# A pair-product batch norm on one core: joining two neighbouring short rows in one tile, beside two long rows in one space of 152 pairs

## The chip, the cores and the metric

The kernel runs on one core of one Trainium2 chip. The time is the device time of that core in microseconds, the median of several runs. The kernel before takes 1864.45 us (three runs, 1864.28 to 1864.72); its profiled run has a span of 1862.7 us. A core has five engines that the profile names: PE (TensorE, matrix products), DVE (VectorE), ACT (ScalarE), POOL (GpSimd) and SP (SyncE, which here only issues transfers), and 16 DMA engines that move data between HBM and the on-chip memory.

## The reference

There are two inputs, xi and xj, each of 1024 samples, 39 fields and 16 numbers. A *pair* (r, c) has a row r from 1 to 38 and a column c from 0 to r - 1, 741 in all; row r has r pairs. For each pair and sample the outer product of xj[r] and xi[c] is formed, 16 x 16 numbers. It is normalised with the mean and variance of that pair over all samples, scaled by gamma and beta, and multiplied by a 16 x 16 weight W:

```python
_ROWS, _COLS = np.tril_indices(39, k=-1)
cross = xj[:, rows, :, None] * xi[:, cols, None, :]
mean = jnp.mean(cross, axis=(0, 2, 3), keepdims=True)
var = jnp.mean(jnp.square(cross - mean), axis=(0, 2, 3), keepdims=True)
normed = (cross - mean) * jax.lax.rsqrt(var + BN_EPS)
normed = normed * gamma[None, :, None, None] + beta[None, :, None, None]
out = normed[:, :, None, :, :] * W[None, None, :, :, :]
return jnp.transpose(out, (0, 2, 1, 3, 4))
```

The output has 1024 x 741 x 256 float32 numbers, 777 MB. In it the pairs of a row follow each other, and row r + 1 follows row r, so for one sample a row is one run of r KB, and two neighbouring rows are one run too.

## The kernel before, in words

**Layout.** A partition of the 128 holds 8 samples (NT = 8). A tile is one row r for T = 2 of them: 2r pairs of 256 numbers, so 2r KB in each partition. All output passes through one buffer, y_sb, of 152 pairs (152 KB in each partition), cut in two halves of 76 (`half`). A tile is laid out sample by sample: the r pairs of sample 0, then the r pairs of sample 1.

**Order of the tiles** (the list `tiles`, lines 68 to 77; an entry is row, first sample, place in y_sb). First row 19, four tiles of 38 pairs. Then row 20, then rows 38 down to 21. A long row r and its partner, the short row 38 - r, have 38 pairs together and fill one half: the long tile at the start of the half, the short one behind it. The halves take turns. So the order is long, short, long, short, and a place is used again after one further half.

**Statistics.** Sums and products of sums over all samples give mean and variance of all pairs without forming the outer products; this takes the first 25 us or so and is not touched. It leaves for each pair a factor s and an offset t, in groups of rows (`ROW_GROUPS`; `apply` prepares a group when a given tile is reached).

**One tile.** `scale_xi` (line 164, POOL) multiplies the r columns of xi by s. `products` (line 178) forms the outer products: for a long enough row one instruction for each sample and each of the 16 values i of xj, most of them on ACT (12 of 16, or 13, or 11 for rows over 33) and the others on POOL, all at line 148 or 150. Rows 5 to 7 are done by POOL in one instruction for each sample (line 203), rows 1 to 4 by DVE (lines 183 and 193). `finish` (line 271) adds t and multiplies by W, one DVE instruction for each pair and both samples (line 308); POOL does a share of the pairs (lines 294 and 297, for rows over 33 with ACT's help at line 292). `store` (line 220) issues the transfers, line 231, all from SP. Rows of up to 19 pairs leave as one transfer for both samples. Longer ones leave as one transfer for each sample; rows over 30 send the first sample in two pieces, the first when its pairs are done (`bounds`, line 262); rows 37 and 38 send the first piece for both samples at once.

**What sets the order.** The program's own order on each engine, written out by the loop at line 521: for tile n it emits `scale_xi` of n + 2, `finish` of n and `products` of n + 1. An instruction that writes pairs of y_sb waits until the earlier transfers that read those same pairs have landed. That is how a new tile waits for the old contents of its place, sample by sample: the places, not the order alone, decide which transfers it waits for.

Of the kernel before, what the change touches and what calls it, by code (L numbers as in the profile page):

```python
# [7 lines left out]
F32 = mybir.dt.float32  # L8
# [6 lines left out]
T = 2  # L15
# [16 lines left out]


ROW_GROUPS = (
    (19, 20, 0, None), (20, 21, 1, None), (18, 19, 1, 2), (38, 39, 1, 8), (34, 38, 1, 9), (1, 5, 1, 10), (29, 34, 2, 36),
    (5, 10, 2, 37), (25, 29, 3, 76), (10, 14, 3, 77), (21, 25, 4, 108), (14, 18, 4, 109),
)
SHORT_GROUP = 5

# [2 lines left out]
def tile_pair_outer_batchnorm(  # L42
# [24 lines left out]

    half = T * (F - 1)
    mid = (F - 1) // 2
    tiles = [(mid, t0, t0 // T * half // 2) for t0 in range(0, NT, T)]  # L70
    slot = 0
    for r in (mid + 1, *range(F - 1, mid + 1, -1)):
        for t0 in range(0, NT, T):
            tiles.append((r, t0, slot * half))
            if r < F - 1:
                tiles.append((F - 1 - r, t0, slot * half + T * r))
            slot ^= 1

    RAW = 1

# [55 lines left out]
    stt = nc.vector.scalar_tensor_tensor  # L136

    def view(n):
        r, _, u = tiles[n]
        return y_sb[:, u : u + T * r, :].rearrange("p (t n) e -> p t n e", t=T)  # L140

    def product(n, engine, t, i, src):

        r, t0, _ = tiles[n]
        y = view(n).rearrange("p t n (i j) -> p t n i j", j=E)[:, t, :, i, :]
        scale = xj_sb[:, t0 + t, r, i : i + 1]
        if engine is nc.scalar:
            nc.scalar.activation(y, src, AF.Copy, scale=scale)  # L148
        else:
            engine.tensor_scalar(y, src, scale, 1.0, ALU.mult, ALU.mult)  # L150

    def raw_products(n, engine, steps):
        r, t0, _ = tiles[n]
        for step in steps:
            t, i = divmod(step, E)
            yield lambda t=t, i=i: product(n, engine, t, i, xi_sb[:, t0 + t, 0:r, :])

    def emit(work, count):
        for _, step in zip(range(count), work):
# [2 lines left out]
    xs_of = {}  # L162

    def scale_xi(n):
        r, t0, _ = tiles[n]
        if r <= SHORT:
            return
        n0 = first[r]
        xs = scaled.tile([P, T, r, E], F32, tag="xs", name=f"xs_{r}_{t0}")
        nc.gpsimd.tensor_tensor(  # L170
            xs,
            xi_sb[:, t0 : t0 + T, 0:r, :],
            s_sb[:, :, n0 : n0 + r, :].to_broadcast([P, T, r, E]),
            ALU.mult,
        )
        xs_of[n] = xs

    def products(n):

        r, t0, _ = tiles[n]  # L180
        if r <= SHORT:
            xs = scaled_short.tile([P, T, r, E], F32, tag="xs_short", name=f"xs_{r}_{t0}")
            nc.vector.tensor_tensor(  # L183
                xs,
                xi_sb[:, t0 : t0 + T, 0:r, :],
                s_short[:, first[r] : first[r] + r]
                .unsqueeze(1)
                .unsqueeze(3)
                .to_broadcast([P, T, r, E]),
                ALU.mult,  # L190
            )
            for t in range(T):
                nc.vector.tensor_tensor(  # L193
                    view(n)[:, t].rearrange("p n (i j) -> p n i j", j=E),
                    xs[:, t].unsqueeze(2).to_broadcast([P, r, E, E]),
                    xj_short[:, t0 + t, r - 1 : r, :].unsqueeze(3).to_broadcast([P, r, E, E]),
                    ALU.mult,
                )
            return
        xs = xs_of.pop(n)  # L200
        if r <= OUTER:
            for t in range(T):
                nc.gpsimd.tensor_tensor(  # L203
                    view(n)[:, t].rearrange("p n (i j) -> p n i j", j=E),
                    xs[:, t].unsqueeze(2).to_broadcast([P, r, E, E]),
                    xj_sb[:, t0 + t, r : r + 1, :].unsqueeze(3).to_broadcast([P, r, E, E]),
                    ALU.mult,
                )
            return
        if n < 3:  # L210
            split = E - POOL_I_FIRST[n]
        elif r > LONG:
            split = E - POOL_I_LONG
        else:
            split = E - (POOL_I_BESIDE if SHORT < F - 1 - r <= OUTER else POOL_I)
        for t in range(T):
            for i in range(E):
                product(n, nc.scalar if i < split else nc.gpsimd, t, i, xs[:, t])

    def store(n, c0, c1, t_from=0, t_to=T):  # L220
        r, t0, _ = tiles[n]
        n0 = first[r]

        whole = n >= len(FIRST_PIECES) and r <= WHOLE
        step = 1 if r > mid and (whole or c1 == r) else t_to - t_from
        for t in range(t_from, t_to, step):
            if whole and step == 1 and t == t_to - 1:
                if c1 < r:
                    continue
                c0 = 0  # L230
            nc.sync.dma_start(  # L231
                out_v[:, t0 + t : t0 + t + step, (n0 + c0) * EE : (n0 + c1) * EE],
                view(n)[:, t : t + step, c0:c1, :].rearrange("p t n e -> p t (n e)"),
            )

    def affine(n, pairs, engines=(nc.scalar, nc.gpsimd)):

        r = tiles[n][0]
        y = view(n)
        for c in pairs:  # L240
            s_c = st_sb[:, 0, first[r] + c : first[r] + c + 1]
            t_c = t_sb[:, first[r] + c : first[r] + c + 1]
            engine = engines[c % len(engines)]
            if engine is nc.scalar:
                nc.scalar.activation(y[:, :, c, :], y[:, :, c, :], AF.Identity, bias=t_c, scale=s_c)  # L245
            else:
                engine.tensor_scalar(y[:, :, c, :], y[:, :, c, :], s_c, t_c, ALU.mult, ALU.add)  # L247
# [14 lines left out]
    def bounds(n):  # L262
        if n < len(FIRST_PIECES):
            return FIRST_PIECES[n]
        r = tiles[n][0]
        if r <= ONE:
            return 0, r

        return 0, r // 2 + max(0, (WHOLE + 1 - r) * 3 // 2), r

    def finish(n):


        r = tiles[n][0]
        n0 = first[r]
        y = view(n)
        long = r > LONG
        p1 = r // 2 if long else r
        if long:
            share = POOL_PAIRS_LONG  # L280
        elif RAW < n < 10:
            share = POOL_PAIRS_FIRST
        else:
            share = int(r * POOL_SHARE + 0.5) if r > SHORT else 0
        p0 = p1 - share
        step = POOL_PAIRS_LONG // 2 if long else r
        for c0 in range(p0, p1, step):
            c1 = min(c0 + step, p1)
            for c in range(c0, c1):
                t_c = t_sb[:, n0 + c : n0 + c + 1]  # L290
                if long:
                    nc.scalar.activation(y[:, :, c, :], y[:, :, c, :], AF.Identity, bias=t_c)  # L292
                else:
                    nc.gpsimd.tensor_scalar(  # L294
                        y[:, :, c, :], y[:, :, c, :], t_c, 1.0, ALU.add, ALU.mult
                    )
            nc.gpsimd.tensor_tensor(  # L297
                y[:, :, c0:c1, :],
                y[:, :, c0:c1, :],
                w_sb.unsqueeze(1).to_broadcast([P, T, c1 - c0, EE]),  # L300
                ALU.mult,
            )

        size = 1 if n == RAW else T
        for t in range(0, T, size):
            for c0, c1 in zip(bounds(n), bounds(n)[1:]):
                for c in [*range(c0, min(c1, p0)), *range(max(c0, p1), c1)]:
                    stt(  # L308
                        y[:, t : t + size, c, :],
                        y[:, t : t + size, c, :],  # L310
                        t_sb[:, n0 + c : n0 + c + 1],
                        w_dve.to_broadcast([P, size, EE]),
                        ALU.add,
                        ALU.mult,
                    )
                store(n, c0, c1, t, t + size)

    with tc.manual_schedule():
# [159 lines left out]
        used = [0] * len(ps_st)  # L478

        def spread(group):  # L480
            r0, r1, bank, _ = ROW_GROUPS[group]
            n0, n1 = first[r0], first[r1 - 1] + r1 - 1
            at = used[bank]
            used[bank] = at + 2 * (n1 - n0)
# [33 lines left out]
        products(1)  # L518
        scale_xi(2)

        for n in range(1, len(tiles)):
            if n + 2 < len(tiles):
                scale_xi(n + 2)
            finish(n)
            for group, (_, _, _, tile_of) in enumerate(ROW_GROUPS):
                if n == tile_of:
                    apply(group)
            if n + 1 < len(tiles):
                products(n + 1)
            if n == 12:  # L530
                nc.scalar.copy(xj_short, xj_sb[:, :, 1 : SHORT + 1, :])
# [28 lines left out]
```

## Time and profile before

| | kernel before |
|---|---|
| time, median of 3 | 1864.45 us |
| span of the profiled run | 1862.7 us |
| DVE busy | 1714.3 us, 92% |
| ACT busy | 1576.3 us, 85% |
| POOL busy | 1542.9 us, 83% |
| written to HBM | 776.99 MB |
| DMA packets | 55286, mean 421 GB/s |
| ACT at line 148 waiting for a transfer out | 181.6 us, 82 times |

The page cuts the span in 40 slices of 46.6 us. A digit is the busy share of an engine, or of the 16 DMA engines, in tenths; the row GB/s is what the DMA moved. In the waits, a line says who waited for whom, the sum in us, how often, and the longest. In the timeline a line has the start, the length, the engine, the line, the operation with its shapes and how many instructions are merged; what stands in brackets is the idle time before it and who ended it. A packet is one run of bytes that one DMA engine moves, here nearly always one run of one sample.

### The profile page before, as it was taken

The numbers are of one execution on the slowest core, as the hardware profiler recorded it, in microseconds if no ns is written. First come the engines' busy times: TensorE is split into PE (matmuls) and PEld (weight loads), VectorE is DVE, ScalarE is ACT, GpSimd is POOL, SyncE is SP. The second block draws the span as 40 slices with busy tenths as digits, with TensorE's granted clock in tenths as the row PEclk, the third lists the DMA queues.
The fourth block names the chain that finished last, engine by engine and source line by source line (L and its number), as shares of the span: only waits on it lengthen the run. The fifth ranks groups of instructions, "written<-read, shape, count | busy, mean of one in ns | idle before, by whom it ended". The sixth has DMA issues, their size and how long they took to land.

```text
span 1862.7 us, 9385 instructions
## 1 busy us (share of the span) xinstructions
PE 34.3 (2%) x212; PEld 33.7 (2%) x212; DVE 1714.3 (92%) x2638; ACT 1576.3 (85%) x3130; POOL 1542.9 (83%) x1655
## 2 busy tenths in 40 slices
PE   7000000000000000000000000000000000000000
PEld 7000000000000000000000000000000000000000
DVE  8999889899999999999999999999999999999994
ACT  8999888888888776666898989999999998989891
POOL 9999777787777789999988888888888888888882
PEclk7555555555555555555555555555555555555555
DMA  7999999999999999999999999999999999999998
GB/s 289 396 421 421 430 427 427 429 424 427 424 428 423 424 424 426 427 425 425 420 428 429 428 430 427 426 427 427 427 431 427 426 428 431 428 425 428 428 428 359
DMA packets 55286, 783.60 MB, mean 421 GB/s; under 512 B 4784, under 2 KB 6448, under 8 KB 18096
## 3 DMA queue, kind: packets, MB, share of 16 engines
q1 hardware_dynamic: 54928, 782.53, 99.2%
q14 instruction: 69, 0.57, 0.1%
q10 hardware_dynamic: 288, 0.48, 0.1%
q8 instruction: 1, 0.02, 0.0%
HBM read 6.00 MB, written 776.99 MB: 420 GB/s over the span
## 4 chain that ended last, share of the span: by engine, by line
DMA 53%; ACT 22%; DVE 18%; issue 3%; POOL 1%; PE 0%; SPq 0%; ACTq 0%; DVEq 0%; POOLq 0%
DMA out_dram<-y_sb 53%; ACT y_sb L148 22%; DVE y_sb L308 17%; POOL y_sb L150 1%; DVE y_sb L364 0%; POOL xs L170 0%; POOL y_sb L247 0%; PE ps L401 0%; SPq L231 0%; DVE y_sb L254 0%; ACTq L148 0%; PE ps L379 0%; DVE y_sb L385 0%; DVE y_sb L371 0%; DVE xs L183 0%
## 5 line engine op out<-in xcount | busy, mean ns | idle before, releaser
L308 DVE SCALAR_TENSOR_TENSOR y_sb<-y_sb,st_sb,w_dve 128x512 f32<-128x512 f32 (+1 forms) x2511 | 1653.1, 740 | 113.3 <-issue 95.9
L148 ACT ACTIVATE y_sb<-xs,xj_sb 128x144 f32<-128x144 f32 (+23 forms) x2930 | 1453.0, 586 | 238.2 <-DMA out_dram<-y_sb 181.6
L297 POOL TENSOR_TENSOR y_sb<-y_sb,w_sb 128x2048 f32<-128x2048 f32 (+3 forms) x155 | 517.4, 3343 | 89.1 <-ACT y_sb L292 79.5
L150 POOL TENSOR_SCALAR y_sb<-xs,xj_sb 128x320 f32<-128x320 f32 (+19 forms) x1006 | 557.4, 577 | 9.8 <-DMA out_dram<-y_sb 9.7
L170 POOL TENSOR_TENSOR xs<-xi_sb,st_sb 128x640 f32<-128x640 f32 (+33 forms) x135 | 183.9, 1362 | 178.8 <-ACT y_sb L148 174.5
L294 POOL TENSOR_SCALAR y_sb<-y_sb,st_sb 128x512 f32<-128x512 f32 x291 | 196.8, 692 | 5.1 <-ACT y_sb L148 5.1
L292 ACT ACTIVATE y_sb<-y_sb,st_sb 128x512 f32<-128x512 f32 x160 | 100.2, 708 | 3.8 <-POOL y_sb L150 2.1
L203 POOL TENSOR_TENSOR y_sb<-xs,xj_sb 128x1280 f32<-128x1280 f32 (+2 forms) x24 | 66.7, 2802 | 0.0
L193 DVE TENSOR_TENSOR y_sb<-xs,ps 128x256 f32<-128x256 f32 (+3 forms) x32 | 24.8, 818 | 0.5
L487 PE MATMUL ps<-y_sb 38*128 38x38 f32 (+37 forms) x76 | 16.4, 397 | 2.4 <-DVE y_sb L473 2.4
L487 PEld LDWEIGHTS ps<-y_sb 38*128 38x128 f32 x76 | 16.3, 329 | 2.5 <-POOL y_sb L150 2.5
L150 POOL TENSOR_SCALAR y_sb<-xi_sb,xj_sb 128x304 f32<-128x304 f32 x24 | 11.9, 514 | 0.0
L254 DVE TENSOR_TENSOR y_sb<-y_sb,w_dve 128x2048 f32<-128x2048 f32 (+4 forms) x6 | 10.8, 1840 | 0.5 <-POOL y_sb L247 0.5
L364 DVE TENSOR_REDUCE y_sb<-y_sb 128x38 f32<-128x608 f32 x14 | 10.4, 781 | 0.0
L247 POOL TENSOR_SCALAR y_sb<-y_sb,st_sb 128x512 f32<-128x512 f32 x9 | 7.0, 786 | 2.2 <-ACT y_sb L148 2.2
L245 ACT ACTIVATE y_sb<-y_sb,st_sb 128x512 f32<-128x512 f32 x9 | 6.5, 803 | 0.3 <-ACT y_sb L148 0.3
L361 ACT ACTIVATE y_sb<-xi_sb 128x608 f32<-128x608 f32 x8 | 5.7, 707 | 1.1 <-DMA xi_sb<-in_r_xi_dram 0.7
L361 ACT ACTIVATE y_sb<-xj_sb 128x608 f32<-128x608 f32 x8 | 5.7, 708 | 1.1 <-DMA xj_sb<-in_r_xj_dram 0.6
L379 PE MATMUL ps<-xi_sb,y_sb 128*128 128x152 f32 x40 | 6.1, 302 | 0.0
L379 PEld LDWEIGHTS ps<-xi_sb,y_sb 128*128 128x128 f32 x40 | 5.8, 202 | 0.0
L401 PE MATMUL ps<-y_sb 128*128 128x128 f32 x24 | 5.5, 428 | 1.0 <-POOL y_sb L319 1.0
L401 PEld LDWEIGHTS ps<-y_sb 128*128 128x128 f32 x24 | 5.2, 331 | 1.0 <-POOL y_sb L319 1.0
(43 smaller groups left out, 50.5 us busy)
## 6 DMA issues: line engine op xcount, KB each, us to landing
out_dram<-y_sb SPq DMA_DIRECT2D x16, 3072.0 KB, 21.9
out_dram<-y_sb SPq DMA_DIRECT2D x20, 2432.0 KB, 12.5
out_dram<-y_sb SPq DMA_DIRECT2D x10, 4608.0 KB, 15.2
out_dram<-y_sb SPq DMA_DIRECT2D x12, 3840.0 KB, 20.8
out_dram<-y_sb SPq DMA_DIRECT2D x16, 2816.0 KB, 22.1
out_dram<-y_sb SPq DMA_DIRECT2D x12, 3584.0 KB, 22.9
out_dram<-y_sb SPq DMA_DIRECT2D x12, 3328.0 KB, 24.3
out_dram<-y_sb SPq DMA_DIRECT2D x15, 2560.0 KB, 12.3
```

The costliest lines, as they stand in the source:

```text
L148: nc.scalar.activation(y, src, AF.Copy, scale=scale)
L150: engine.tensor_scalar(y, src, scale, 1.0, ALU.mult, ALU.mult)
L170: nc.gpsimd.tensor_tensor(xs, xi_sb[:, t0 : t0 + T, 0:r, :], s_sb[:, :, n0 : n0 + r, :].to_broadcast([P, T, r, E]), ALU.mult,)
L193: nc.vector.tensor_tensor(view(n)[:, t].rearrange("p n (i j) -> p n i j", j=E), xs[:, t].unsqueeze(2).to_broadcast([P, r, E, E]), xj_short ...
L203: nc.gpsimd.tensor_tensor(view(n)[:, t].rearrange("p n (i j) -> p n i j", j=E), xs[:, t].unsqueeze(2).to_broadcast([P, r, E, E]), xj_sb[:, ...
L292: nc.scalar.activation(y[:, :, c, :], y[:, :, c, :], AF.Identity, bias=t_c)
L294: nc.gpsimd.tensor_scalar(y[:, :, c, :], y[:, :, c, :], t_c, 1.0, ALU.add, ALU.mult)
L297: nc.gpsimd.tensor_tensor(y[:, :, c0:c1, :], y[:, :, c0:c1, :], w_sb.unsqueeze(1).to_broadcast([P, T, c1 - c0, EE]), ALU.mult,)
L308: stt(y[:, t : t + size, c, :], y[:, t : t + size, c, :], t_sb[:, n0 + c : n0 + c + 1], w_dve.to_broadcast([P, size, EE]), ALU.add, ALU.mult,)
L361: nc.scalar.activation(squares[x][:, t], sources[x][:, t], AF.Square, scale=scales[x])
L379: nc.tensor.matmul(ps, unit, sources[x][:, t0:t1, :, e : e + q], start=e == 0, stop=e + q == E)
L487: nc.tensor.matmul(ps[:, :, first[r] - n0 : first[r] - n0 + r], pick[:, r - 1, :], stq[:, :, 0:r], start=True, stop=True,)
```

## The change

From row 37 down the tiles go in rounds of three for each two samples: the long row r (r odd), the long row r - 1, and one tile of both their partners, the short rows 38 - r and 39 - r, which are neighbours. A round has 2r + 2(r - 1) + 2(77 - 2r) = 152 pairs, the whole of y_sb: r at the start, r - 1 at the end, the joined tile between them. The joined tile leaves as one run of 77 - 2r pairs for each sample, where two rows left as two runs. Rows 20, 18 and 38 stay as they were. Row 21, which is left over, goes with row 17, two tiles of each at a time. The aim is fewer and longer runs in the stores. In the functions an entry of `tiles` now holds a tuple of rows, `parts` walks through them, `bounds` gives a joined tile one piece, POOL's share of pairs is taken of the joined tile's sum, and the tiles at which `apply` runs are worked out instead of listed.

```diff
-    tiles = [(mid, t0, t0 // T * half // 2) for t0 in range(0, NT, T)]
+    tiles = [((mid,), t0, t0 // T * half // 2) for t0 in range(0, NT, T)]
     slot = 0
-    for r in (mid + 1, *range(F - 1, mid + 1, -1)):
+    for r in (mid + 1, F - 1):
         for t0 in range(0, NT, T):
-            tiles.append((r, t0, slot * half))
+            tiles.append(((r,), t0, slot * half))
             if r < F - 1:
-                tiles.append((F - 1 - r, t0, slot * half + T * r))
+                tiles.append(((F - 1 - r,), t0, slot * half + T * r))
             slot ^= 1
+    for r in range(F - 2, mid + 2, -2):
+        for t0 in range(0, NT, T):
+            tiles.append(((r,), t0, 0))
+            tiles.append(((r - 1,), t0, 2 * half - T * (r - 1)))
+            tiles.append(((F - 1 - r, F - r), t0, T * r))
+    r = mid + 2
+    for t0 in range(0, NT, 2 * T):
+        tiles.append(((r,), t0, 0))
+        tiles.append(((r,), t0 + T, 2 * half - T * r))
+        tiles.append(((F - 1 - r,), t0, T * r))
+        tiles.append(((F - 1 - r,), t0 + T, T * (F - 1)))
...
     def view(n):
-        r, _, u = tiles[n]
-        return y_sb[:, u : u + T * r, :].rearrange("p (t n) e -> p t n e", t=T)
+        rows, _, u = tiles[n]
+        return y_sb[:, u : u + T * sum(rows), :].rearrange("p (t n) e -> p t n e", t=T)
+
+    def parts(n):
+        at = 0
+        for r in tiles[n][0]:
+            yield r, at, at + r
+            at += r
...
+        for r, c0, c1 in parts(n):
...
             for t in range(T):
-            for i in range(E):
-                product(n, nc.scalar if i < split else nc.gpsimd, t, i, xs[:, t])
+                for i in range(E):
+                    engine = nc.scalar if i < split else nc.gpsimd
+                    product(n, r, c0, engine, t, i, xs[:, t, c0:c1])

     def store(n, c0, c1, t_from=0, t_to=T):
-        r, t0, _ = tiles[n]
-        n0 = first[r]
+        rows, t0, _ = tiles[n]
+        n0, r = first[rows[0]], sum(rows)
...
-        r = tiles[n][0]
-        if r <= ONE:
+        rows = tiles[n][0]
+        r = sum(rows)
+        if r <= ONE or len(rows) > 1:
             return 0, r
...
-            share = int(r * POOL_SHARE + 0.5) if r > SHORT else 0
+            share = int(r * POOL_SHARE + 0.5) if rows[-1] > SHORT else 0
...
+        due = {}
+        for group, (r0, r1, _) in enumerate(ROW_GROUPS[2:], 2):
+            use = min(n for n, tile in enumerate(tiles) if any(r0 <= r < r1 for r in tile[0]))
+            due.setdefault(use - 3 if group == 2 else use - 4, []).append(group)
```

## The prediction

> **What bounds the kernel now.** I read the busy times and the slices of the page first, then the waits, then two DMA windows, then the timeline of single tiles.
>
> ```profile
> PE 34.3 (2%) x212; PEld 33.7 (2%) x212; DVE 1714.3 (92%) x2638; ACT 1576.3 (85%) x3130; POOL 1542.9 (83%) x1655
> ...
> DMA  7999999999999999999999999999999999999998
> GB/s 289 396 421 421 430 427 427 429 424 427 424 428 423 424 424 426 427 425 425 420 428 429 428 430 427 426 427 427 427 431 427 426 428 431 428 425 428 428 428 359
> ...
> HBM read 6.00 MB, written 776.99 MB: 420 GB/s over the span
> ```
>
> DVE's 92% is not the limit: from the second slice to the last but one the DMA row is full, at 420 to 431 GB/s. 777 MB must leave, so the stores set the end. The waits agree: the engines wait for landed stores, not the stores for a late engine.
>
> ```profile
> ACT y_sb L148 <- DMA out_dram<-y_sb: 181.6, 82, 6.7
> POOL xs L170 <- ACT y_sb L148: 174.5, 67, 6.3
> DVE y_sb L308 <- issue: 95.9, 66, 5.0
> ```
>
> So the change can act in two ways: cheaper bytes on a full DMA, or a DMA that runs empty. For the first, compare the DMA between 312 and 915 us (rows 37 to 31, whose first sample leaves in two pieces) with that between 930 and 1830 us (rows 30 to 21, whole runs):
>
> ```profile
> DMA packets 18561, 256.80 MB, mean 426 GB/s; under 512 B 1664, under 2 KB 2432, under 8 KB 8832
> ...
> DMA packets 21715, 385.01 MB, mean 428 GB/s; under 512 B 1856, under 2 KB 1856, under 8 KB 1856
> ```
>
> Leaving out the completion packets of 4 B (under 512 B), these are 65.8 packets per MB at 2.348 us per MB against 51.6 at 2.338. The slope is 0.74 ns of the whole DMA per packet (11.9 ns on one of 16 engines), the rest 2.299 us per MB, 435 GB/s.
>
> For the second, the timeline of ACT, with long tiles of rows 31 and then 30:
>
> ```profile
> 841.56 7.90 ACT L148 ACTIVATE y_sb<-xs,xj_sb 128x496 f32<-128x496 f32 x13 [6.74 <-DMA out_dram<-y_sb]
> 850.71 7.89 ACT L148 ACTIVATE y_sb<-xs,xj_sb 128x496 f32<-128x496 f32 x13 [1.24 <-DMA out_dram<-y_sb]
> 864.41 7.90 ACT L148 ACTIVATE y_sb<-xs,xj_sb 128x496 f32<-128x496 f32 x13 [5.82 <-DMA out_dram<-y_sb]
> 873.69 7.90 ACT L148 ACTIVATE y_sb<-xs,xj_sb 128x496 f32<-128x496 f32 x13 [1.37 <-DMA out_dram<-y_sb]
> ```
>
> One tile is two lines, one for each sample. ACT computes sample 0 (7.9 us) as soon as the old sample 0 of that place has landed, and waits only 1.2 to 1.4 us more for the old sample 1. **Half of the products are hidden under the landing of the second sample.** That matters because little else is spare: the trace puts the issues of the first piece of rows 33 to 30 only 2.4 to 4.3 us before the preceding store lands.
>
> **The Trainium skill.** "DMA: Bandwidth & Descriptors", section "Where 436 GB/s comes from", gives 435.2 GB/s as the ceiling of the SBUF ports; my fit gives 435, the run 428. The same page, "Why small descriptors are slow", has a fixed overhead per packet; the fit agrees in kind, 11.9 ns. Its section "Why a DMA increments its semaphore by 16 and not by 1" says that only the full count means that all has landed, so a waiter is released by the slowest of 16 engines; here 12 engines end at 1854.5 us and the last at 1861.1. "Latency and other measured facts" has some 0.6 us to the first byte of a store from these queues; here the first store's data started 0.9 us after its issue, and the last store landed 0.43 us after its last byte.
>
> **Prices from the trace.** ACT L148 start to start: 0.305 us at 9 pairs, 0.319 at 10, 0.532 at 26, 0.559 at 28, 0.572 at 29, 0.586 at 30, 0.613 at 32, 0.639 at 34. A DVE L308 step takes 0.658 us. A store lands 0.3085 us after the one before it for each pair of a sample (24 pairs in 7.41 us).
>
> ```profile
> 1511.33 18.52 DVE L308 SCALAR_TENSOR_TENSOR y_sb<-y_sb,st_sb,w_dve 128x512 f32<-128x512 f32 x28
> 1511.70 19.68 ACT L148 ACTIVATE y_sb<-xs,xj_sb 128x224 f32<-128x224 f32 x44
> ```
>
> **The change part by part.** Call the three tiles of a round A (row r), B (row r-1) and C (the two short rows), and a stage the four rounds of one r.
>
> 1. *Joined runs.* In eight stages each sample has one short packet where it had two: 8 x 1024 = 8192 packets fewer, x 0.74 ns = 6.1 us. 20 stores fewer, each with a 9 ns completion packet per engine: 0.2 us. Upper end 6.3. Lower end 0: the slowest engine's landings take 93.8 us per 304 pairs in both windows. But that engine also carries 8 KB instruction packets of 0.31 us, more of them in the second window, so I take 6 us.
>
> 2. *Same engine work.* Instruction counts hardly move (four DVE steps more, four POOL ones fewer, 24 fewer POOL multiplications in L297). Engines wait for stores; I cost this at nothing.
>
> 3. *C as one tile.* Its products can't start before its store has landed (both samples in one store up to 19 pairs, row after row above). In the stage 29/28 the chain is: C landed, products of rows 9 and 10 (24 x 0.305 + 24 x 0.319 = 15.0), products of A (24 x 0.572 = 13.7), its 25 DVE steps (16.4), 1.7 us of latencies: 46.8 us. Available: one round, 152 pairs, 46.7 to 46.9. So no margin, 0 to 1.4 us lost twice; I take 1. For 23/22 the same sum leaves about 5 us.
>
> 4. *The place of B.* A starts at 0 and shrinks within its old place, but B ends at 152: it starts at 152 - 2(r-1), and from stage to stage its start moves up by 4 pairs. Old row 36: sample 0 in pairs 80 to 116, sample 1 to 152. New row 34: sample 0 in pairs 84 to 118. **The new sample 0 lies 2 pairs deep in the old sample 1.** In the built program the first product of row 34 indeed waits for the stores of pairs 80-99, 99-116 and 116-152, while later rounds wait only for their own sample; the same for rows 32, 30, 28, 26, 24, 22. So in the first round of a stage nothing of B is computed until all of the old B has landed. Behind the waiting ACT instruction stand C and the next A; POOL's share of B waits too, then DVE, then the store queue.
>
> Count from the landing of the old B. The DMA still has the old C and the new A: W. B needs its products P, the DVE (or, for row 34, L292 and POOL) part F of its first store, and 1.67 us of latencies (landing 0.43, starts 0.2, issue 0.14, first byte 0.9).
> - Row 34: W = 76 x 0.3085 = 23.4; P = 22 x 0.639 = 14.1; F = 4 x 0.613 + 2 x 4.48 (L297) = 11.4. Empty 3.7.
> - Row 32: W = 80 pairs, 24.7; P = 26 x 0.613 = 15.9; F = 23 x 0.658 = 15.1. Empty 8.1.
> - Row 30: W = 84 pairs, 25.9; P = 24 x 0.586 = 14.1; F = 26 x 0.658 = 17.1. Empty 6.9.
> - Row 28: W = 88 pairs, 27.1; 13.4 + 15.8. Empty 3.7.
> - Row 26: W = 92 pairs, 28.4; 12.8 + 15.1. Empty 1.2.
> - Rows 24 and 22: 2 and 5 us to spare. Row 36: the old row 38 stores its first 19 pairs for both samples at once and has the overlap anyway; nothing new.
>
> Sum 23.6 us. The same arithmetic on the kernel before (row 23: 12.3 us of slack worked out, 12.1 in the trace) holds, but for rows 30 to 33 it is 0.2 to 1.2 us too kind, so I add 2: 25.6. Bounds 21 to 29.
>
> Sum: -6 + 1 + 25.6 = +20.6: 1864.45 + 20.6 = **1885**.
>
> **The rivals.** (a) *Faster*: the DMA stays full at the turns of stage and only the packets count: 1864.45 - 6 = 1858.5. For it speaks the full DMA row; against it the waits of the built program, and that the stores of the kernel before have little lead. 6%. (b) *Half*: part of the empty time is caught up, 12 us lost and 6 gained: 1870. Against it: nothing but A and C is queued. 9%, of which 4% so close to the time before that it counts as the same. (c) *The joined C becomes the bound*: step 3 fails by 2 us in each round of the last four stages, and the turns come on top: 1885 + 30 = 1915, or with half of it 1900. Against it: 3 us or more of margin outside 29/28. 7%. My forecast has 78%.
>
> The range takes in the bounds of the two unknown costs: gain 6.3 and loss 21 to 22 give 1879, gain 0 and loss 29 give 1893; a bit of (b) moves the lower end to 1875. Faster 0.06, same 0.04, slower 0.90.
>
> **What will show it.** Right: DMA gaps of 4 to 9 us just ahead of the first store of rows 34, 32, 30 and 28, and after ACT has waited for a store at the start of those tiles with no second wait between the samples; DMA full in between, with about a quarter fewer packets per MB and some 1.5 GB/s more. Wrong: a full DMA row with no gaps (a), or gaps in every round of the late stages (c). The prediction falls if stores land earlier than I reckon at the turn, or if packets turn out to cost the slowest engine nothing.

## The result and the profile after

The changed kernel takes **1892.14 us** (median of four runs, 1891.93 to 1892.22) against 1864.37 us for the kernel before on the same chip: a ratio of 1.0149, interval [1.0131, 1.0167]. That is 27.8 us slower; the forecast was 1885, 20.6 us slower.

First the page of the changed kernel, with the same rows as were shown of before.

```profile
PE 33.1 (2%) x212; PEld 32.3 (2%) x212; DVE 1714.0 (91%) x2642; ACT 1572.9 (83%) x3130; POOL 1530.2 (81%) x1627
...
DMA  7999999999899989998999899999999999999999
GB/s 296 396 422 424 425 426 415 428 428 432 363 433 422 427 342 429 425 423 360 433 429 426 383 421 428 419 414 428 430 429 423 431 429 430 408 428 429 428 428 388
DMA packets 46774, 783.60 MB, mean 415 GB/s; under 512 B 4464, under 2 KB 5104, under 8 KB 12656
```

No engine has more to do: DVE has 1714.0 us where it had 1714.3. But the DMA row has four 8s, and the GB/s row falls to 363, 342, 360 and 383 in just these slices, four apart. A slice is 47.3 us and a stage of four rounds of 152 pairs about 190 us, so the holes come once in a stage. Between them the rate is 422 to 433, about what it was.

The next view is a table by stretches: after the start and end come length, busy time of PE, PEld, DVE, ACT and POOL, granted clock, DMA share and GB/s. The stretches are the holes, found in the records of the packets, and one of 100 us well away from them.

```profile
476.00:482.00 6.00, 0.00 (x0) 0.00 (x0) 6.00 (x10) 6.00 (x11) 6.00 (x3) 0.50 0.15 65
668.00:678.00 10.00, 0.00 (x0) 0.00 (x0) 10.00 (x16) 10.00 (x17) 10.00 (x5) 0.50 0.09 39
863.00:871.00 8.00, 0.00 (x0) 0.00 (x0) 8.00 (x13) 8.00 (x15) 8.00 (x10) 0.50 0.09 38
1055.00:1061.00 6.00, 0.00 (x0) 0.00 (x0) 6.00 (x10) 6.00 (x17) 5.92 (x13) 0.50 0.12 48
1500.00:1600.00 100.00, 0.00 (x0) 0.00 (x0) 93.78 (x144) 86.03 (x198) 83.68 (x107) 0.50 1.00 429
```

In the holes the DMA is at a tenth and DVE, ACT and POOL are busy all the time: the DMA has run out of stores while the engines make the next one. What they were late for is in the timeline of ACT around the turn of stage at which row 32 takes the place of row 34.

```profile
645.04 16.02 ACT L165 ACTIVATE y_sb<-xs,xj_sb 128x512 f32<-128x512 f32 x26 [12.39 <-DMA out_dram<-y_sb]
663.23 16.39 ACT L165 ACTIVATE y_sb<-xs,xj_sb 128x528 f32<-128x528 f32 x26 [2.17 <-POOL xs L188]
687.84 8.07 ACT L165 ACTIVATE y_sb<-xs,xj_sb 128x512 f32<-128x512 f32 x13 [8.21 <-DMA out_dram<-y_sb]
697.59 8.08 ACT L165 ACTIVATE y_sb<-xs,xj_sb 128x512 f32<-128x512 f32 x13 [1.67 <-DMA out_dram<-y_sb]
```

An instruction of 512 elements is row 32, of 528 row 33. The first tile of row 32 waits once, for 12.39 us, and then both samples run in one line of 26. One round later the same row waits 8.21 us, does sample 0 (13 instructions), and waits again for 1.67 us. So only the first round of the stage loses the overlap of products and landing.

**The account of the DMA.** From the packets I take for each kernel the time that the 16 engines were without a packet, as a mean over the engines ("idle"), and the rest of the span ("busy"). The trace doesn't say which engine moved a packet, so at each moment I count the packets in flight, 16 at most, as the engines at work. Span 1862.7 us before is 1838.4 busy and 24.3 idle; 1890.4 after is 1833.2 busy and 57.2 idle. The packets saved 5.2 us, and 32.9 us of idle came in: 28.8 us in five holes (5.3 ahead of row 34, 8.8 of row 32, 7.4 of row 30, 5.3 of row 28, 2.1 of row 26), 2.3 us at 1632 us ahead of the first joined tile of the stage 23/22, and 1.8 us net in small stretches, the end of the run among them. (Where packets overlap, more than 16 are in flight. Without the limit of 16 the saving would be 7.1 us.)

### The profile page after: what moved, and what is told of

Same layout as the page of the kernel before. It is cut to its first block, busy times and chain, and to the rows that moved or that the text cites. A ratio compares the mean times of both kernels' runs of the same rounds, so it can differ in the third digit from the quotient of the medians.

```text
span 1890.4 us, 9242 instructions
## 1 busy us (share of the span) xinstructions
PE 33.1 (2%) x212; PEld 32.3 (2%) x212; DVE 1714.0 (91%) x2642; ACT 1572.9 (83%) x3130; POOL 1530.2 (81%) x1627
## 5 line engine op out<-in xcount | busy, mean ns | idle before, releaser
L165 ACT ACTIVATE y_sb<-xs,xj_sb 128x576 f32<-128x576 f32 (+23 forms) x2930 | 1449.8, 587 | 268.6 <-DMA out_dram<-y_sb 219.0
L319 POOL TENSOR_TENSOR y_sb<-y_sb,w_sb 128x2048 f32<-128x2048 f32 (+2 forms) x131 | 508.4, 3888 | 88.2 <-ACT y_sb L314 80.6
L167 POOL TENSOR_SCALAR y_sb<-xs,xj_sb 128x320 f32<-128x320 f32 (+21 forms) x1006 | 556.9, 577 | 21.8 <-DMA out_dram<-y_sb 17.7
```

Source lines behind the costliest of these rows:

```text
L319: nc.gpsimd.tensor_tensor(y[:, :, c0:c1, :], y[:, :, c0:c1, :], w_sb.unsqueeze(1).to_broadcast([P, T, c1 - c0, EE]), ALU.mult,)
```

## The experiments

All ratios are against the kernel before on the same chip; it took 1864.0 to 1864.4 us throughout. The summary first, with the account of the DMA:

| kernel | us | ratio, interval | data packets | DMA busy | DMA idle |
|---|---|---|---|---|---|
| before | 1864.37 | 1 | 50176 | 1838.4 | 24.3 |
| after | 1892.14 | 1.0149 [1.0131, 1.0167] | 41984 | 1833.2 | 57.2 |
| 1 B's samples exchanged | 1871.51 | 1.0038 [1.0024, 1.0052] | 41984 | 1833.1 | 36.6 |
| 2 as 1, joined tile as two runs | 1874.21 | 1.0053 [1.0040, 1.0066] | 50176 | 1838.5 | 33.9 |
| 3 before, long rows at the end | 1905.16 | 1.0218 [1.0204, 1.0232] | 50176 | 1838.9 | 64.5 |
| 4 as 1, row 38 stores sample 1 first | 1865.40 | 1.0007 [0.9999, 1.0015] | 41984 | 1833.0 | 30.6 |
| 5 as 4, joined tile sample by sample | 1864.98 | 1.0005 [0.9997, 1.0013] | 41984 | 1832.7 | 30.6 |
| 6 as 5, joined tile as two runs | 1869.45 | 1.0029 [1.0018, 1.0039] | 50176 | 1838.3 | 29.4 |
| 7 as 5, joined transfers cut at partition 64 | 2246.26 | 1.2052 [1.2009, 1.2094] | 41984 | 2118.6 | 121.7 |
| 8 before, rows 21 to 26 in one transfer | 1863.17 | 0.9995 [0.9987, 1.0003] | 50176 | 1838.7 | 22.4 |
| 9 as 5, rows 21 to 25 in one transfer | 1864.65 | 1.0002 [0.9994, 1.0010] | 41984 | 1832.8 | 29.8 |
| 10 even partitions only | 2517.94 | 1.3507 [1.3488, 1.3525] | 24192 | 1109.6 | 1406.2 |
| 11 before, half of the DVE steps | 1861.93 | 0.9988 [0.9982, 0.9995] | 50176 | 1837.9 | 22.2 |
| 12 as 5, half of the DVE steps | 1858.09 | 0.9967 [0.9955, 0.9980] | 41984 | 1831.7 | 24.3 |

**The theories.** Theory 1: the turns of stage make the loss, because the new sample 0 of B reaches into the old sample 1. Rival: the joined tile, or the order of long, long, joined, makes it. Both are tested by moving places only.

**1. B's samples exchanged.** B's sample 0 now lies behind its sample 1 in y_sb. The order of work is unchanged, but the new sample 0 lies within the old sample 0.

```diff
+            flip.add(len(tiles))
             tiles.append(((r - 1,), t0, 2 * half - T * (r - 1)))
...
+    def place_of(n, t):
+        return T - 1 - t if n in flip else t
...
-        y = view(n)[:, t, at : at + r].rearrange("p n (i j) -> p n i j", j=E)[:, :, i, :]
+        y = view(n)[:, place_of(n, t), at : at + r].rearrange("p n (i j) -> p n i j", j=E)[:, :, i, :]
...
+            at = place_of(n, t)
...
-                view(n)[:, t : t + step, c0:c1, :].rearrange("p t n e -> p t (n e)"),
+                view(n)[:, at : at + step, c0:c1, :].rearrange("p t n e -> p t (n e)"),
```

> The changed kernel with one thing different: tile B keeps its place at the end of the space, but sample 0 lies behind sample 1, so that the new sample 0 lies wholly within the old sample 0 at every turn of stage. Theory (the turns cost, because the new sample 0 of B reaches into the old sample 1): the gaps ahead of rows 34, 32, 30, 28 and 26, 28.8 us in the trace of the changed kernel, go; what stays is the smaller ones (about 3 us) and the gain of the joined runs (about 5 us): 1862 us, 1858 to 1866. Rival (the space has three tiles where it had four, and the DMA runs empty for that): the time stays near 1892, with gaps at the same places. Rival (half the turn is the wait, half the larger round): near 1878.

It took 1871.51 us, 20.6 us less than the changed kernel, and missed its expectation of 1862 by 9.5 us. The packets show why: the holes at the turns are gone (from 304 to 1068 us none is over 1 us), and one has come at 290 us. The table of stretches has two of the old places and the new one.

```profile
476.00:482.00 6.00, 0.00 (x0) 0.00 (x0) 6.00 (x10) 4.89 (x8) 6.00 (x2) 0.50 0.98 419
668.00:678.00 10.00, 0.00 (x0) 0.00 (x0) 10.00 (x16) 8.08 (x13) 9.84 (x7) 0.50 0.88 373
289.00:297.00 8.00, 0.00 (x0) 0.00 (x0) 8.00 (x14) 8.00 (x13) 8.00 (x3) 0.50 0.19 81
```

ACT waits twice again in the first round of row 32:

```profile
635.00 8.08 ACT L171 ACTIVATE y_sb<-xs,xj_sb 128x512 f32<-128x512 f32 x13 [2.14 <-DMA out_dram<-y_sb]
645.10 8.07 ACT L171 ACTIVATE y_sb<-xs,xj_sb 128x512 f32<-128x512 f32 x13 [2.01 <-DMA out_dram<-y_sb]
```

The new hole (6.3 us) is the same fault at another place. A small hole of 0.9 us behind it, which the expectation of number 4 counts with it, is not of this kind: the changed kernel has it too (at 296 us). Row 36 comes after row 38, which stores its first 19 pairs for both samples, then the rest of sample 0, then that of sample 1. The exchange puts row 36's sample 0 over the piece that leaves last.

**2. The joined tile in two runs.** To the kernel of 1, the two rows of a joined tile leave by a transfer each, as they did before.

```diff
-            nc.sync.dma_start(
-                out_v[:, t0 + t : t0 + t + step, (n0 + c0) * EE : (n0 + c1) * EE],
+            cuts = [(a, b) for _, a, b in parts(n)] if len(rows) > 1 else [(c0, c1)]
+            for a, b in cuts:
+                nc.sync.dma_start(
+                    out_v[:, t0 + t : t0 + t + step, (n0 + a) * EE : (n0 + b) * EE],
```

> The kernel of e1_swap with the join undone in the store alone: the joined tile is computed as one tile but leaves as two transfers, one for each of its rows, so two runs for each sample as in the kernel before: 8192 more packets and 32 + 32 more transfers. Theory (a packet costs 0.74 ns of the whole DMA): 6 us more than e1_swap, 5 to 7.5. Rival (the slowest DMA engine does not feel the packets, or the overhead is hidden): the same as e1_swap within 1 us.

It took 1874.21 us, 2.7 us more than 1 and not 6. DMA busy did rise by 5.4 us, but idle fell by 2.7. So the busy time rose about as forecast (0.66 ns per packet for 0.74), but half of it was taken from idle time; the result lies between theory and rival. This became the second question, taken up in 5 and after.

**3. The fault put into the kernel before.** Only places differ from the kernel before: from row 37 down the long tile lies at the end of its half instead of at the start. Its start then moves up by 2 pairs per row. Order, packets and joining stay as before.

```diff
-            tiles.append((r, t0, slot * half))
+            short = F - 1 - r if r > mid + 1 else 0
+            tiles.append((r, t0, slot * half + T * short))
             if r < F - 1:
-                tiles.append((F - 1 - r, t0, slot * half + T * r))
+                tiles.append((F - 1 - r, t0, slot * half + (0 if short else T * r)))
```

> The kernel before, no tile joined and the order as it was, with one thing different from row 37 down: within its half the short tile comes first and the long tile ends at the end of the half, so that at each turn of row the new long sample 0 reaches into the old sample 1. Theory: a gap at the turn of each row from 36 to 28, by the same sum 2 to 7 us each and 38 us in all, mostly once for the two halves: 1900 us, 1890 to 1915. Rival (the overlap is harmless while there are four places, or costs nothing at all): 1864 us, within 3.

It took 1905.16 us, 40.8 us more, for nothing but places. Holes came at rows 35 to 27, where rows 36 to 28 were expected (none at 36, 1.5 us at 27). Here are two of them, the first with the stretches on either side:

```profile
640.00:648.00 8.00, 0.00 (x0) 0.00 (x0) 7.79 (x12) 1.16 (x3) 7.65 (x6) 0.50 0.93 393
648.00:656.00 8.00, 0.00 (x0) 0.00 (x0) 8.00 (x13) 8.00 (x14) 7.84 (x6) 0.50 0.15 61
656.00:664.00 8.00, 0.00 (x0) 0.00 (x0) 6.58 (x11) 7.35 (x12) 5.36 (x8) 0.50 0.96 406
749.00:757.00 8.00, 0.00 (x0) 0.00 (x0) 8.00 (x13) 8.00 (x15) 7.84 (x6) 0.50 0.14 61
```

In ACT's timeline the first tile of row 33 has all its 26 products in one piece, the second has 13 and a wait:

```profile
646.96 16.40 ACT L149 ACTIVATE y_sb<-xs,xj_sb 128x528 f32<-128x528 f32 x26 [6.84 <-DVE y_sb L309]
666.58 8.25 ACT L149 ACTIVATE y_sb<-xs,xj_sb 128x528 f32<-128x528 f32 x13 [3.22 <-DMA out_dram<-y_sb]
```

The arithmetic of step 4 (the time that the DMA still has, less products, first store and latencies), worked out for these turns, gives for each row the first of two numbers, and the second is the idle time measured: row 35 2.8 and 3.3 us, 34 1.9 and 3.0, 33 6.6 and 7.4, 32 6.2 and 7.0, 31 5.9 and 6.7, 30 5.1 and 5.5, 29 3.5 and 4.0, 28 1.9 and 3.1, 27 0.3 and 1.5. It gets the order of the rows right and is 0.4 to 1.2 us short each time. Idle outside these holes hardly changed (64.5 - 41.5 = 23.0, 24.3 before).

**4. The first turn mended.** To the kernel of 1, the last tile of row 38 sends the second piece of sample 1 ahead of that of sample 0.

```diff
-        for t in range(t_from, t_to, step):
+        late = rows == (F - 1,) and t0 == NT - T and step == 1
+        for t in range(t_from, t_to, step)[:: -1 if late else 1]:
```

> The kernel of e1_swap, where one new gap of 6.3 us stood ahead of the first row 36, because the swapped sample 0 there lies over the sample that row 38 stores last. Here the last tile of row 38 stores the second piece of its sample 1 before that of its sample 0; nothing else differs. Theory of the turns: that gap and the 0.9 us behind it go, the rest stays: 1865 us, 1864 to 1867. Rival (the gap comes from the change of plan there, not from the samples' order): 1871.5.

It took 1865.40 us, 26.7 us less than the changed kernel with the same tiles, instructions and packets. The hole of 6.3 us ahead of row 36 is gone, while the small one behind it stays (0.9 us at 296 us): the stretch from 289 to 297 us has a DMA share of 0.84 where it had 0.19.

```profile
289.00:297.00 8.00, 0.00 (x0) 0.00 (x0) 7.96 (x15) 8.00 (x13) 8.00 (x10) 0.50 0.84 355
```

So places explain the loss, and the rival falls: the joined tile and the order, with the gain of the joined runs taken off, cost 1.3 us (1864.07 before, in the same set of runs). What is left open is the other half: DMA busy is 5.4 us below that of before, and the time is not.

**5 and 6. The joined tile by samples, as one run and as two.** In 5 a joined tile from rows 5 and 6 up is computed sample by sample and stored by one transfer for each, so that the next one can start on sample 0 early. Number 6 is 5 with the cut of number 2.

```diff
+        for some in ((0,), (1,)) if joined else (range(T),):
+          for r, c0, c1 in parts(n):
...
-                for t in range(T):
+                for t in some:
...
-        step = 1 if r > mid and (whole or c1 == r) else t_to - t_from
+        step = 1 if joined or r > mid and (whole or c1 == r) else t_to - t_from
```

> The kernel of e4_first_turn, with the joined tile (from rows 5 and 6 on) computed sample after sample instead of row after row, and stored as one transfer for each sample, so that its first sample can begin when the old first sample has landed. Theory (step 3: the joined tile's products start too late, and the small gaps of the stages 29/28 and 23/22 eat the gain of the joined runs): 2 to 4 us less than e4_first_turn, 1862 us, and then faster than the kernel before. Rival (those gaps only idle engines that are ahead of the slowest one): the same as e4_first_turn within 1 us.

> The kernel of e5_by_sample, with the joined tile leaving as two runs for each sample, one for each row. Theory (a packet costs 0.65 to 0.74 ns of the whole DMA where the DMA is never without work; e2_two_runs showed only 2.7 us since its baseline still had gaps that ate the rest): 5 to 6 us more than e5_by_sample. Rival (the slowest engine feels half of it): 2 to 3 us more.

Number 5 took 1864.98 us, 0.4 less than 4: its first theory missed by 3 us, the rival held. Number 6 took 4.5 us more than 5, between its two theories, with 5.6 us more DMA busy. Thus joining is worth 4.5 us inside this schedule, and the schedule without joining (6) is 5.4 us worse than before. Number 5 has the busy time that was hoped for and 6.3 us more idle than before. Much of it is in one stretch:

```profile
1590.00:1600.00 10.00, 0.00 (x0) 0.00 (x0) 10.00 (x16) 10.00 (x22) 7.80 (x6) 0.50 1.01 431
1600.00:1606.00 6.00, 0.00 (x0) 0.00 (x0) 5.91 (x10) 6.00 (x13) 5.92 (x10) 0.50 0.17 73
1606.00:1616.00 10.00, 0.00 (x0) 0.00 (x0) 10.00 (x16) 9.29 (x20) 9.92 (x12) 0.50 1.06 455
```

The next store, the first joined tile of the stage 23/22, was issued at 1605.3 us; the store before it landed at 1609.0. By the landings it came 3.7 us early, and still the DMA share is 0.17 for 6 us, without a moment in which all 16 engines are idle. Twelve of the 16 engines had counted their part as landed by 1600.9 us, and the slowest followed 8.1 us later. A landing is that of the slowest engine (the Trainium skill, "DMA: Bandwidth & Descriptors", section "Why a DMA increments its semaphore by 16 and not by 1": only the full count means that all has landed), so **a lead measured from landings overstates what the fast engines have**.

What made this store late is in the timeline of DVE:

```profile
1587.27 25.28 DVE L343 SCALAR_TENSOR_TENSOR y_sb<-y_sb,st_sb,w_dve 128x512 f32<-128x512 f32 x38 [4.00 <-issue]
```

A DVE step takes a pair of both samples. ACT ended row 15's products of sample 1 at 1587.2 us, and the first 27 of these 38 steps, those of the joined tile, then ran until 1605.2, just before the issue. Computing by samples puts the products of sample 1 last, and so held DVE up here, where in 4 it did not wait. The small holes of 4 in the stages 29/28 to 23/22, 6.3 us in sum, are gone in 5, but this one (4.7 us) and 1.6 us more at the end stand in their place. So the time that the rival gave came out, and its reason is not shown.

That gave two theories for the missing 5 us. Lateness: stores come too late for the engines that are ahead. Transfers: the slowest engine, whose landings took 0.308 to 0.309 us per pair from 300 to 1550 us both before and in 5, pays for each transfer and not for each packet (number 6 has 56 more, and 4.5 / 56 = 0.08 us).

**7. Transfers doubled, packets kept.** To the kernel of 5, each joined transfer is cut into partitions 0 to 63 and 64 to 127.

```diff
+            half_p = P // 2 if len(rows) > 1 else P
+            for p in range(0, P, half_p):
...
-                out_v[:, t0 + t : t0 + t + step, (n0 + c0) * EE : (n0 + c1) * EE],
-                view(n)[:, at : at + step, c0:c1, :].rearrange("p t n e -> p t (n e)"),
+                    out_v[p : p + half_p, t0 + t : t0 + t + step, (n0 + c0) * EE : (n0 + c1) * EE],
+                    view(n)[p : p + half_p, at : at + step, c0:c1, :].rearrange("p t n e -> p t (n e)"),
```

> The kernel computed sample by sample with its joined runs (1864.98 us, 272 transfers), with one thing changed: each transfer of a joined tile is cut in two by partitions, 64 and 64, so that the data packets stay as few and as long and only the number of transfers rises by 56 to 328, as many as with two runs per sample (1869.45 us). If what counts is the number of transfers (0.06 to 0.08 us each): +3.4 to +4.5 us, 1868.4 to 1869.5. If what counts is the number of data packets (0.55 ns each): only the completion packets are added, 56 x 16 x 0.55 ns = 0.5 us, 1865.5. Between 1866.3 and 1867.6 both would have a part.

It took 2246 us (its runs lie between 2232 and 2275), far from both theories, and answers another question. Its DMA row and rate:

```profile
DMA  7999999999998999999999999998999999998997
GB/s 305 410 427 419 428 405 420 408 410 368 364 356 330 380 367 364 358 386 378 378 365 353 355 320 296 345 352 313 306 308 291 265 301 302 307 291 240 304 379 337
```

The DMA is full and moves as little as 240 GB/s: the packets themselves are slow. Packets of 31 KB took 1.18 us in 5; here the upper tenth took 2.64 us or more, and half of all over 2.0. Until near the end the rate falls to the right, where the joined tiles are larger.

**10. Even and odd partitions.** Meant as 7 with the cut made between even and odd partitions.

```diff
-                    out_v[p : p + half_p, t0 + t : t0 + t + step, (n0 + c0) * EE : (n0 + c1) * EE],
+                    out_v[p::2, t0 + t : t0 + t + step, (n0 + c0) * EE : (n0 + c1) * EE],
-                    view(n)[p : p + half_p, at : at + step, c0:c1, :].rearrange("p t n e -> p t (n e)"),
+                    view(n)[p::2, at : at + step, c0:c1, :].rearrange("p t n e -> p t (n e)"),
```

> As the kernel with joined transfers cut in two by partitions, but with the even partitions in one transfer and the odd ones in the other, so that each transfer reads from the whole width of y_sb. Halves of 64 neighbouring partitions moved at about half the rate (a 31 KB packet took 2.0 to 2.6 us in place of 1.18), which hid what the number of transfers costs. If even and odd partitions keep the full rate: 1868.4 to 1869.5 us if transfers count at 0.06 to 0.08 us each, 1865.5 if only packets count, beside 1864.98 with whole transfers. If the half rate comes from the number of partitions and not from their place: again over 2200 us.

The edit did something else than was meant: `p` runs over 0 and 64. All stores left out the odd partitions, and the second transfer of a joined tile wrote partitions 64, 66 to 126 a second time, each after waiting for the first. The 2517.94 us are the time of that, with the DMA idle for 1406 us, and say nothing on the number of transfers. One reading is of use: packets of 26 KB, all from transfers of 64 even partitions, took 0.994 us, as in 5 (0.992), with 16 packets in flight, while of 31 KB, where a third of the joined packets come from 32 even partitions in the upper half alone, the upper tenth took 2.48 us or more. So it is not the number of 64 partitions that makes them slow; where they lie does.

**8 and 9. Fewer transfers.** In 8, the kernel before, and 9, the kernel of 5, the rows from 21 up to 26 and 25 leave by one transfer for both samples.

```diff
-        step = 1 if r > mid and (whole or c1 == r) else t_to - t_from
+        both = n >= len(FIRST_PIECES) and mid + 1 < r < 27
+        step = 1 if not both and r > mid and (whole or c1 == r) else t_to - t_from
```

In 9 the samples of tile B also keep their plain order from row 24 down, as its expectation says.

> The kernel before (1864.1 to 1864.5 us, 280 transfers), with rows 21 to 26 leaving as one transfer for both samples in place of one for each: 24 transfers fewer, the same data packets. If transfers count at 0.06 to 0.08 us each: -1.4 to -1.9 us, about 1862.5. If data packets count: -0.2 us, 1864. A rise of over 1 us would mean that the store now comes too late or lands too late for the next tile, shown by gaps in the DMA.

> The kernel computed sample by sample with its joined runs (1864.98 us, 272 transfers), with the tiles of rows 21 to 25 leaving as one transfer for both samples (252 transfers; the second long tile of a round keeps its samples in their plain order there). If transfers count at 0.06 to 0.08 us each: -1.2 to -1.6 us, about 1863.5, the lowest time so far. If data packets count: -0.2 us, 1864.8. A rise of over 1 us would mean late stores, shown by gaps.

They took 1863.17 us (0.9 less than before) and 1864.65 (0.3 less than 5). Neither reaches the 1.2 to 1.9 us that the price per transfer asks for, neither is clear of no change, and number 8 lies between its two theories. A small price per transfer isn't excluded; one of 0.06 to 0.08 us finds no support.

**11 and 12. Early stores.** Every second DVE step is left out, in the kernel before and in that of 5. The data that leave are as many as ever.

```diff
                 for c in [*range(c0, min(c1, p0)), *range(max(c0, p1), c1)]:
+                    if n > RAW and c % 2:
+                        continue
```

> The kernel before, with every second DVE step of finish (odd columns, all tiles after the first) left out: those pairs leave without offset and W. DVE's work falls by nearly half, so that stores come well ahead of the DMA. If the stores of the kernel before are early enough for all 16 DMA engines already: 1863 to 1864.5 us, no more than 1 us under the kernel before. It is the base for the next kernel.

> The kernel computed sample by sample with joined runs, with the same DVE steps left out as in the kernel before it in this list. Theory 1, the gain of 8192 fewer packets is lost because stores come too late for the DMA engines that are ahead of the slowest: with early stores it appears, 4 to 6 us under the other thinned kernel, about 1859. Theory 2, the slowest DMA engine doesn't gain by fewer packets: within 1 us of the other thinned kernel, about 1864. In between, 1861 to 1862: both.

They took 1861.93 and 1858.09 us: with early stores the joined kernel is 3.8 us the faster, where with late ones it had no lead. Number 11 missed its own expectation (1863 to 1864.5): it is 2.3 us under the kernel before, with 2.1 us less idle, so some stores of that kernel came late for some engines too. Of the theories for number 12, the second said within 1 us and falls; the first said 4 to 6 and got nearly that. From both pages, first 11 and then 12:

```profile
DVE  8554344455555444444454544445544454444441
...
DMA packets 55276, 783.52 MB, mean 421 GB/s; under 512 B 4784, under 2 KB 6448, under 8 KB 18096
```

```profile
DVE  8554345544555554445454444444544444444452
...
DMA packets 46957, 783.52 MB, mean 422 GB/s; under 512 B 4656, under 2 KB 5296, under 8 KB 12848
```

DVE is at half in both. The median lead, the time from a store's issue to the landing of the store before it, is 18.2 us in 11 and 15.9 in 12 for the stores after 60 us (11.0 before, 9.3 in 5). Idle is 22.2 and 24.3 us, so of 6.2 us saved in busy time 2.1 are lost: the hole of 4.7 us has shrunk to 0.5, and 1.6 us more stand at the end, where the engines wait for the slowest.

## Why the prediction was right, step by step

**The cause was right, and shown.** Step 4 (the place of B) carried the forecast. Number 4 takes the overlap away and with it 26.7 us, number 3 puts it into the kernel before and adds 40.8 us, and the timelines show the one long wait that step 4 described. Holes came at rows 34, 32, 30, 28 and 26 and none over 1 us at 36, 24 and 22, as written. Joining itself did not make the kernel slower. The range held with 1 us to spare, and in part by luck: its upper end, 1893, put a gain of 0 with a loss of 29, and measured were a gain of 5.2 and 32.9 us of new idle time.

**The miss of 7 us, by terms.** The sum was -6 + 1 + 25.6 = 20.6 us. The traces give -5.2 (packets) + 28.8 (turns) + 2.3 (the first joined tile of 23/22) + 1.8 (small stretches, those of 29/28 among them, and the end) = 27.7 us.

- *Step 1, joined runs, 6 us.* Nearly so: busy time fell by 5.2 us, or 0.63 ns of the whole DMA per packet for 0.74 foreseen. I had put the lower end at 0 because the slowest engine's landings seemed not to care. Without the limit of 16 it is 7.1 us, 0.87 ns. In 4 and 5 the saving was taken back as idle time.
- *Step 2, engine work, nothing.* Right: DVE -0.3 us, ACT -3.4, POOL -12.7.
- *Step 3, C as one tile, 1 us.* Too small, and for 23/22 by the wrong path. In the stage 29/28, where I saw no margin, three holes (1090, 1137 and 1184 us) of 0.3 to 0.9 us make 1.8 us. In 23/22, where I saw 5 us of margin, 2.3 us are lost ahead of the first joined tile. Its products had waited only 0.34 us for a landing (ACT at 1608.3 us); DVE was late. It worked without a pause, and its last 27 steps are the joined tile:

```profile
1603.46 30.38 DVE L330 SCALAR_TENSOR_TENSOR y_sb<-y_sb,st_sb,w_dve 128x512 f32<-128x512 f32 x46 [2.11 <-issue]
1616.10:1634.00 17.90, 0.00 (x0) 0.00 (x0) 17.73 (x27) 17.90 (x41) 12.64 (x15) 0.50 0.90 382
```

The second line is that stretch in the table's columns. The joined tile leaves in one piece, so its stores come after all 27 steps, at 1634.0 us, 17.4 us after the last one of row 22. Row 22 gave the DMA 44 pairs to move, 13.6 us at the price of the prediction. Step 3 had the wait for the landing and the next tile A, but not the joined tile's own DVE steps ahead of its own store.

- *Step 4, turns, 25.6 us.* Mis-sized by 3.2 us. Foreseen were 3.7, 8.1, 6.9, 3.7 and 1.2, and 2 for kindness; idle was 5.3, 8.8, 7.4, 5.3 and 2.1. Here too I counted from the landing. The time with all 16 engines idle is 4.3, 8.3, 6.5, 4.0 and 1.6 us, 24.6 in sum, close to the 23.6 that the formula gave. The other 4.2 us are those of engines that had finished ahead of the slowest. Idle at the end fell from 7.1 to 4.0 us. That holes let the slowest engine catch up there is not shown: number 4, without the five holes, has 3.9 us at the end.

**The rivals.** (a), only packets count, and (b), caught up by half, fail: no hole was made good later, the 3.1 us at the end apart. (c), the joined tile as bound in each round, fails: number 4 has the joined tile and loses 1.3 us, and its holes in the late stages are of 0.3 to 1.8 us.

**What stays open.** Whether a transfer has a small price of its own isn't settled: 7 and 10 changed something else as well, 8 and 9 are inside the uncertainty. No kernel that does all the work beat the kernel before measurably. Numbers 11 and 12 say that joining is worth some 4 us when stores come earlier than DVE lets them here. A way to that without leaving work out, such as a joined tile that leaves in two pieces, is not tried.

## What to carry to other kernels

When tiles of changing size share a buffer, draw the new tile over the old one part by part: the first part to be written should lie only over what leaves first. A tile that shrinks toward its far end breaks this without any change in order or work, and exchanging the places of its two parts mends it; look also at the turn before, where the mend can make the same fault. A joined tile that leaves in one piece puts the steps of both its parts ahead of one store: compare them with the time that the stores queued before it give the DMA. Count spare time of a full DMA from when its fast engines run dry, not from the landing, or a saving in packets can turn into idle time.

## What the runs showed of the hardware

- The busy time of the DMA falls into two groups: 1837.9 to 1838.9 us in the kernels with 50176 data packets, 1831.7 to 1833.2 in those with 41984 (7 and 10 apart). Between the kernels of a pair (before and after, 1 and 2, 5 and 6, 8 and 9, 11 and 12) it is 5.2 to 6.2 us, so by estimate a packet costs 10 to 12 ns of its engine (x 16 / 8192). A straight line through the median packet times of 5, from 3 to 36 KB, gives about 11 ns and 37.7 ns per KB. The Trainium skill ("DMA: Bandwidth & Descriptors", section "Why small descriptors are slow") has a fixed overhead per packet; the runs agree that there is one, in packets as long as these.
- A store from 64 neighbouring partitions kept all 16 engines busy at about half the rate each (31 KB: 2.0 to 2.6 us for 1.18). One from 64 even partitions, also with 16 packets in flight, had packets of the usual length (26 KB: 0.994 us for 0.992). The runs don't show what is shared.
- In a stream of stores that had kept all 16 engines busy, the slowest landed 8.1 us after twelve others had (number 5 at 1600 us).
